# A state-space layer on VectorE: the next group's product with B placed in front of the last scan

## The chip, the cores and the metric

The kernel runs on one core of one Trainium2 chip. The metric is the device time of one execution in microseconds (us). Before the change it is 19662.92 us, the median of three runs (19660.62 to 19663.58).

## The reference, cut to what matters

The network has four layers, each added to its input after a group norm. The change touches only layer 1, which runs two mamba blocks one after the other over 65536 positions (256 x 256), for two images with 64 channels each, 128 inner channels and 16 states:

```python
dA = jnp.exp(jnp.einsum('bld,dn->bldn', delta, A))
dBu = jnp.einsum('bld,bln,bld->bldn', delta, Bm, u)

def step(h, xs):
    dA_t, dBu_t, C_t = xs
    h = dA_t * h + dBu_t
    return (h, jnp.einsum('bdn,bn->bd', h, C_t))
...
y = jnp.moveaxis(ys, 0, 1) + u * D
y = y * _silu(res)
return y @ out_w.T
```

`delta` is a softplus and `u` a Silu of a short convolution. A layer norm follows each block.

## The kernel before, in words

**Steps and groups.** The positions are cut into 128 chunks of 512. A step is one chunk of one mamba block: the list `tasks` alternates the two blocks, the second one three chunks behind the first, and has 256 steps. Within a step there are eight groups (b, j), for the two images b and four state indices j. A group holds four tiles `h[:, k]` of 128 x 512: channels and states are laid out so that one j covers all 128 channels with four of the 16 states. The text calls the groups of a step g0 to g7: g0 to g3 are b=0 with j=0 to 3, g4 to g7 are b=1.

**What a group does.**
- The product with B, delta times u times B, fills `h`. For j = 0, 1 and 3 VectorE makes it (L773) from `dv` (delta times u, fetched from DRAM) and `pb`, a PSUM bank in which TensorE has spread the row of B over the partitions. For j = 2 GpSimd makes it (L755, function `product`) from `cb`, a copy of the B and C rows in SBUF; this is issued at the end of the group three earlier, at j = 3.
- For k = 0 to 3 ScalarE computes `da = exp(delta * A)` into PSUM (L789), and VectorE scans `h[:, k]` in place with it (L792). `da` has three buffers.
- GpSimd keeps the last column as the next state (L795) and multiplies `h` by C (L796).
- TensorE sums over the states into the bank `py` (the matmuls `py<-h`); the function `before` issues these in the fourth scan's place (k = 3) of the following group. `py` has one bank and starts for each half with `u * D`.
- `gate` (L654, VectorE) multiplies `py` of a finished half with `silu(res)`. It is issued in the groups with j = 1, that is in g1 for the second half of the step before and in g5 for the first half of this one.

**What stands around it.** The engines' order is written out by hand (a manual schedule)[...]. At k = 3 of each group, ahead of the fourth `da`, the generator `steps` issues one part of the work for other steps: the front end of the step two ahead (`front`: affine in g0, convolution matmuls in g1 and g2, Silu activations in g3, the matmuls for delta and B, C in g4, softplus, the copy of B and C, GpSimd's `du` (L622) and the spill to DRAM in g5), the fetches of the next step (L641, L645, in g1 and g5), and the layer norm of the step before (`layer_norm`: out projection, square and mean in g6, logarithm and exponential in g7; its VectorE product L673 comes in the next g0, batch statistics of the second block in g1). Exponential, Silu, softplus and logarithm need different activation tables, so ScalarE reloads tables in g3, g5 and g7.

**The bank pb.** `spread` issues the TensorE matmul that fills `pb` for the next direct group, right behind the product that used it:

```python
def spread():
    n, b, j = next(rows, (None, None, None))
    if n is None:
        return None
    pb = p_b.tile([P, T], F32, name="pb")
    mm(pb, sel[:, b, j], ts[n]["bc"])
    return pb
```

`pb` has one bank, `h` five buffers, `dl`, `dv` and `cb` three each. In the profile all these matmuls stand under the helper's line, L561, and are told apart by their tiles.

## Time and profile before

| | |
|---|---|
| median of three runs | 19662.92 us |
| the profiled execution, its own time | 19667.66 us |
| its span | 19665.9 us |
| first to last L773 (layer 1) | 1533.4 to 15696.1 us |
| scans L792 | 8192, 1263 ns each |
| VectorE products L773 | 1536, 2261 ns each |
| gates L654 | 512, 684 ns each |
| exponentials L789 | 8192, 688 ns each |
| GpSimd products L796 / L755 | 2048, 4518 ns / 512, 4529 ns |

The page lists each engine's busy time as a share of the span. In rows of waits the engine and line that waited come first, then what it waited for, the total in us, the number of times and the longest. In the timeline each row has its start, its length, the engine, line and operation with its tiles, how many instructions it joins, and in brackets the idle time before it and what ended it. Start-to-start times are a little shorter than lengths where instructions of one engine overlap.

### The profile page before, as it was taken

The numbers are of one execution on the slowest core, as the hardware profiler recorded it, in microseconds if no ns is written. First come the engines' busy times: TensorE is split into PE (matmuls) and PEld (weight loads), VectorE is DVE, ScalarE is ACT, GpSimd is POOL, SyncE is SP. The second block draws the span as 40 slices with busy tenths as digits, with TensorE's granted clock in tenths as the row PEclk, the third lists the DMA queues.
The fourth block names the chain that finished last, engine by engine and source line by source line (L and its number), as shares of the span: only waits on it lengthen the run. The fifth ranks groups of instructions, "written<-read, shape, count | busy, mean of one in ns | idle before, by whom it ended". The sixth has DMA issues, their size and how long they took to land. (4 is left out here: it accounts for less than half of the span.)

```text
span 19665.9 us, 162715 instructions
## 1 busy us (share of the span) xinstructions
PE 14640.5 (74%) x48720; PEld 4861.7 (25%) x48720; DVE 18472.7 (94%) x16222; ACT 11804.0 (60%) x16810; POOL 16050.1 (82%) x8070
## 2 busy tenths in 40 slices
PE   7996767776777677767777677676777688888886
PEld 3431111111111111111111111111111154444444
DVE  6888999999999999999999999999999989999997
ACT  2226666666666666666666666666666555555554
POOL 6987888888888888888888888888888855555554
PEclk9996666666666666666666666666666698989898
DMA  3116666666666666666666666666666500000004
GB/s 124 54 50 157 151 151 151 153 149 156 149 154 152 151 151 151 155 147 157 151 153 150 151 152 151 156 148 154 154 150 151 126 28 29 30 30 29 29 27 145
DMA packets 662182, 2438.84 MB, mean 124 GB/s; under 512 B 131888, under 2 KB 201264, under 8 KB 450160
## 3 DMA queue, kind: packets, MB, share of 16 engines
q1 hardware_dynamic: 661296, 2428.43, 51.4%
q8 instruction: 385, 6.31, 0.1%
q14 instruction: 501, 4.10, 0.1%
HBM read 1990.14 MB, written 437.78 MB: 123 GB/s over the span
## 5 line engine op out<-in xcount | busy, mean ns | idle before, releaser
L792 DVE TENSOR_TENSOR_SCAN h<-da,st,h 128x512 f32<-128x512 f32 x8192 | 9838.6, 1263 | 308.2 <-ACT da L789 223.3
L796 POOL TENSOR_TENSOR h<-h,cb 128x2048 f32<-128x2048 f32 x2048 | 9253.1, 4518 | 164.9 <-POOL st L795 0.4
L789 ACT ACTIVATE da<-dl,p_a 128x512 f32<-128x512 f32 x8192 | 5565.3, 688 | 3985.5 <-DVE h L792 3891.2
L561 PE MATMUL py<-h,t_c_quad 128*32 128x512 f32 x16384 | 3253.7, 817 | 1649.1 <-POOL h L796 1648.6
L561 PE MATMUL pb<-bc,t_c_sel 64*128 64x512 f32 x3072 | 2697.0, 972 | 2385.5 <-DVE h L773 2379.9
L773 DVE TENSOR_TENSOR h<-dv,pb 128x2048 f32<-128x2048 f32 x1536 | 3472.3, 2261 | 40.9 <-DMA dv<-d_dv 40.9
L1021 POOL TENSOR_TENSOR gl<-gl,prod 128x512 f32<-128x512 f32 x1544 | 1959.0, 1270 | 1498.7 <-ACT prod L1017 1423.3
L755 POOL TENSOR_TENSOR h<-dv,cb 128x2048 f32<-128x2048 f32 x512 | 2318.7, 4529 | 17.1 <-DMA dl<-d_dl 17.1
L980 DVE SCALAR_TENSOR_TENSOR acc<-z,tap_b,acc 128x1024 f32<-128x1024 f32 (+1 forms) x1560 | 1988.4, 1275 | 38.8
L561 PEld LDWEIGHTS pb<-bc,t_c_sel 64*128 64x128 f32 x3072 | 661.6, 267 | 4411.3 <-DVE h L773 4345.9
L795 POOL COPY st<-h 128x4 f32<-128x4 f32 x2048 | 384.1, 188 | 1365.1 <-DVE h L792 1352.7
L561 PEld LDWEIGHTS py<-h,t_c_quad 128*32 128x32 f32 x16384 | 424.0, 122 | 3815.3 <-POOL h L796 3217.3
L561 PE MATMUL mm<-xin,p_conv 64*128 64x512 f32 x4096 | 1322.9, 775 | 15.2 <-DMA x1t<-y 15.2
L1064 PE MATMUL pcv<-z,diag 128*128 128x512 f32 x2322 | 1174.7, 623 | 19.8 <-ACT gl L1072 16.4
L949 ACT COPY z<-pz 128x512 f32<-128x512 f32 x768 | 456.4, 598 | 1034.1 <-PE pz L941 928.7
L1017 ACT ACTIVATE prod<-z,tap_a 128x512 f32<-128x512 f32 x1544 | 1045.1, 714 | 37.0 <-POOL gl L1021 36.8
L941 PE MATMUL pz<-t_c_inv,gf 128*128 128x128 f32 (+1 forms) x8192 | 1039.4, 309 | 1.9 <-DVE gf L922 1.9
L941 PEld LDWEIGHTS pz<-t_c_inv,gf 128*128 128x128 f32 (+1 forms) x8192 | 849.4, 181 | 520.0 <-issue 311.7
L561 PE MATMUL mm<-u,p_dt 128*128 128x512 f32 x1024 | 931.2, 1064 | 0.0
L561 PE MATMUL py<-u,p_d 128*128 128x512 f32 x1024 | 820.8, 894 | 0.0
L915 PE MATMUL f<-t_w_inT,xf 64*128 64x384 f32 x2048 | 596.7, 616 | 155.9 <-DVE gf L922 154.8
L561 PEld LDWEIGHTS mm<-xin,p_conv 64*128 64x128 f32 x4096 | 460.5, 244 | 982.6 <-issue 982.5
(167 smaller groups left out, 17448.8 us busy)
## 6 DMA issues: line engine op xcount, KB each, us to landing
cb<-d_bc SPq DMA_DIRECT2D x2048, 320.0 KB
dl<-d_dl SPq DMA_DIRECT2D x2048, 256.0 KB
dv<-d_dv SPq DMA_DIRECT2D x2048, 256.0 KB
d_dl<-delta SPq DMA_DIRECT2D x256, 512.0 KB
d_dv<-du SPq DMA_DIRECT2D x256, 512.0 KB
xin<-in_x SPq DMA_DIRECT2D x16, 2048.0 KB
xt<-in_x SPq DMA_DIRECT2D x32, 1024.0 KB
y<-yt SPq DMA_DIRECT2D x128, 256.0 KB
```

Of the source, the lines that this page charges most:

```text
L561: nc.tensor.matmul(out, lhsT, rhs, start=start, stop=stop)
L755: nc.gpsimd.tensor_tensor(h, t["dv", b], t["cb", b][:, 0].unsqueeze(1).to_broadcast([P, 4, T]), ALU.mult,)
L773: nc.vector.tensor_tensor(h, t["dv", b], pb.unsqueeze(1).to_broadcast([P, 4, T]), ALU.mult)
L789: nc.scalar.activation(da, t["dl", b][:, k], AF.Exp, scale=ws[m]["a"][:, k, j : j + 1])
L792: nc.vector.tensor_tensor_scan(h[:, k], da, h[:, k], state[m, b][:, j, k : k + 1], ALU.mult, ALU.add)
L796: nc.gpsimd.tensor_tensor(h, h, t["cb", b][:, 1 + j].unsqueeze(1).to_broadcast([P, 4, T]), ALU.mult)
L915: nc.tensor.matmul(p, x_f[t][half, g], w_in[half], start=True, stop=True)
L941: nc.tensor.matmul(pz[i * n : (i + 1) * n, k, :, 16 * g : 16 * g + 16], gf[t, 2 * e + g, b][:, c0 : c0 + n], inv, start=True, stop=True,)
L980: eng.scalar_tensor_tensor(out, near(s, name, m0, r, k), w, box["t"], ALU.mult, ALU.add)
L1017: nc.scalar.activation(prod, near(s, name, 4 * h + m, n, k), AF.Copy, scale=w)
L1021: nc.gpsimd.tensor_add(acc, acc, prod)
L1064: nc.tensor.matmul(box["t"], diag[:, k], near(s, f"a{i}", 4 * h + m, n, k), start=k == 0, stop=k == 8,)
```

## The change

The direct product of a group moves from the head of its own group to the group before it, between the fourth `da` and the fourth scan. It becomes a function, `direct_product`, that also issues the next `spread`; its tile is handed on in the dictionary `ahead`, which the products of j = 2 use already. Groups with j = 1 are followed by j = 2, so nothing is moved into them. The gate moves from the head of the groups with j = 1 to the place in front of their third exponential and scan. On TensorE, the matmuls for `pb` so come behind the `py` matmuls that `before` issues at k = 3. What is computed stays the same.

```diff
--- before.py
+++ after.py
@@ -760,27 +760,29 @@
                     )
                     return h

-                ahead = {2: product(*groups[2])}
+                def direct_product(n, b, j):
+                    nonlocal pb
+                    h = pool.tile([P, 4, T], F32, name="h", bufs=5)
+                    nc.vector.tensor_tensor(
+                        h, ts[n]["dv", b], pb.unsqueeze(1).to_broadcast([P, 4, T]), ALU.mult
+                    )
+                    pb = spread()
+                    return h
+
                 pb, before = spread(), None
+                ahead = {2: product(*groups[2]), 0: direct_product(*groups[0])}
                 for g, (n, b, j) in enumerate(groups):
                     if b == j == 0:
                         steps = aside(n)
                     if j == 0:
                         st = states.tile([P, 4, 4], F32, name=f"st{tasks[n][0]}{b}")
                     t, m = ts[n], tasks[n][0]
-                    if j != 2:
-                        h = pool.tile([P, 4, T], F32, name="h", bufs=5)
-                        nc.vector.tensor_tensor(
-                            h, t["dv", b], pb.unsqueeze(1).to_broadcast([P, 4, T]), ALU.mult
-                        )
-                        pb = spread()
-                    else:
-                        h = ahead.pop(g)
+                    h = ahead.pop(g)
                     if b == j == 0:
                         next(norm, None)
-                    if j == 1 and g > 1:
-                        gate(ts[n - 1 + b], 1 - b)
                     for k in range(4):
+                        if j == 1 and k == 2 and g > 1:
+                            gate(ts[n - 1 + b], 1 - b)
                         if k == 3:
                             next(steps)
                             if before:
@@ -789,6 +791,8 @@
                         nc.scalar.activation(
                             da, t["dl", b][:, k], AF.Exp, scale=ws[m]["a"][:, k, j : j + 1]
                         )
+                        if k == 3 and g + 1 < len(groups) and j != 1:
+                            ahead[g + 1] = direct_product(*groups[g + 1])
                         nc.vector.tensor_tensor_scan(
                             h[:, k], da, h[:, k], state[m, b][:, j, k : k + 1], ALU.mult, ALU.add
                         )
```

## The prediction

> **What bounds the kernel now.** I read the page's busy times first, then the waits inside layer 1 (1533 to 15715 us), then the timeline engine by engine. The page:

> ```profile
> PE 14640.5 (74%) x48720; PEld 4861.7 (25%) x48720; DVE 18472.7 (94%) x16222; ACT 11804.0 (60%) x16810; POOL 16050.1 (82%) x8070
> ```

> VectorE (DVE) is the bound; GpSimd (POOL) is near it. What VectorE waits for in layer 1:

> ```profile
> DVE h L792 <- ACT da L789: 223.3, 357, 1.1
> DVE res L654 <- PE py L561: 202.8, 237, 7.0
> ```

> So about 430 us is all that better order inside VectorE could win. [...] Between the first and last of 254 steps VectorE took (15648.56 - 1642.17) / 253 = 55.36 us a step. One step on VectorE, then ScalarE (ACT), POOL and PE:

> ```profile
> 8015.11 2.26 DVE L773 TENSOR_TENSOR h<-dv,pb 128x2048 f32<-128x2048 f32 x1
> 8017.29 0.68 DVE L654 TENSOR_TENSOR res<-res,py 128x512 f32<-128x512 f32 x1
> 8017.89 9.50 DVE L792 TENSOR_TENSOR_SCAN h<-da,st,h 128x512 f32<-128x512 f32 x8
> 8033.96 1.28 DVE L792 TENSOR_TENSOR_SCAN h<-da,st,h 128x512 f32<-128x512 f32 x1 [0.66 <-ACT da L789]
> 8035.16 2.26 DVE L773 TENSOR_TENSOR h<-dv,pb 128x2048 f32<-128x2048 f32 x1
> 8037.53 4.81 DVE L792 TENSOR_TENSOR_SCAN h<-da,st,h 128x512 f32<-128x512 f32 x4
> 8042.25 2.26 DVE L773 TENSOR_TENSOR h<-dv,pb 128x2048 f32<-128x2048 f32 x1
> 8045.51 0.69 DVE L654 TENSOR_TENSOR res<-res,py 128x512 f32<-128x512 f32 x1 [1.00 <-PE py L561]
> 8046.12 9.50 DVE L792 TENSOR_TENSOR_SCAN h<-da,st,h 128x512 f32<-128x512 f32 x8
> ```

> ```profile
> 8042.37 0.69 ACT L789 ACTIVATE da<-dl,p_a 128x512 f32<-128x512 f32 x1 [0.48 <-DVE h L792]
> 8043.08 1.28 ACT L525 ACT_TABLE_LOAD   x1
> 8046.12 1.28 ACT L789 ACT_TABLE_LOAD   x1
> 8047.43 0.69 ACT L789 ACTIVATE da<-dl,p_a 128x512 f32<-128x512 f32 x1
> ```

> ```profile
> 8035.58 4.52 POOL L796 TENSOR_TENSOR h<-h,cb 128x2048 f32<-128x2048 f32 x1
> 8040.05 4.53 POOL L755 TENSOR_TENSOR h<-dv,cb 128x2048 f32<-128x2048 f32 x1
> 8044.79 4.51 POOL L796 TENSOR_TENSOR h<-h,cb 128x2048 f32<-128x2048 f32 x1
> 8049.26 2.36 POOL L622 TENSOR_TENSOR du<-delta,u 128x1024 f32<-128x1024 f32 x1
> 8051.83 4.50 POOL L796 TENSOR_TENSOR h<-h,cb 128x2048 f32<-128x2048 f32 x1
> ```

> ```profile
> 8056.39 1.94 PE L561 MATMUL py<-h,t_c_quad 128*32 128x512 f32 x8 [1.56 <-POOL h L796]
> 8058.25 2.07 PE L561 MATMUL pb<-bc,t_c_sel 64*128 64x512 f32 x2
> ```

> The waits stand at fixed places. The scan's wait is in the last scan of g3 (165 us of it over the 254 steps), behind ScalarE's Silu work; the rest (56 us) lies in g6. The gate's (194 us) is in g5. The step's other gate, in g1, waits once.

> [...] a direct product D (L773) is followed by its own scan 2.37 us after its start (8035.16, 8037.53), but by the gate, which doesn't read it, after 2.18. [...] in the trace da always waits behind the side work. [...] the pb pair shows both, 2.07 and 1.12 us. [...]

> **The change, part by part.** Nothing is added or removed: a step keeps 32 scans, six D, two gates. Start-to-start on VectorE: scan 1.18 ((9.50 - 1.26) / 7), D 2.18 or 2.37, gate 0.60 (8017.29 to 8017.89), layer-norm product 0.60 likewise, batch statistics 0.60 in every second step (0.30 on average).

> *D in front of the last scan.* Its own scan no longer follows, so each costs 2.18. Before, three of six paid 2.37 (those of g3, g4, g7; others had a gate or L673 behind). Worth 0.57 us a step if nothing waits.

> *Which group has the D as cover.* Between the last scan of a group (s3) and the next s3 stood that group's own D; now it is the next group's. So g2 and g6 gain a D of cover, g1 and g5 lose theirs. ScalarE's da is a ring of three, so its third da waits for the previous s3, and the side work and fourth da come after it. In g5 the side work is the softplus with two table loads. Counted from s3 of g4 (8042.25 - 1.18 = 8041.07), da for the last scan is ready at 8048.15, that is 7.08 later. New VectorE work in that stretch: four scans and the gate, 4.72 + 0.60 = 5.32. New wait 1.76 us. In g3 the Silu side work needs 7.83 (s3 of g2 at 8027.31 - 1.18 = 8026.13, last scan 8033.96) against 6.90: wait 0.93, which eats the 0.19 there. g6 and g7 have 6.90 and need less: ScalarE's side work of g7, from the load of L670 at 8056.37 to the end of L671's activation at 8060.29, makes it about 2.0 + 3.9 + 0.7 = 6.6.

> *The gate two scans down.* py waits for POOL and PE. From s3 of g3 the gate now comes at 6.90 + 3.54 = 10.44 us; POOL's product ends at 6.14 and PE then needs 2 to 4 us at most. The wait goes: 0.76 a step, and 0.08 of overlap that a wait costs.

> *pb and PE's order.* The bank pb is single, and PE loads the next pb behind the D. That matmul was issued at the group's start, ahead of the py matmuls of the group before; now it is issued at the fourth scan, right behind them, and those wait for POOL. The place where it bites is D for the next g0, now in g7: its pb stands behind py of g5. POOL's queue from s3 of g3 is back to back (product, L755, product, du, product: rows above) and ends at 8056.33, 22.37 us after that s3; over 252 steps it lies between 22.35 and 22.39. VectorE can't change it, since POOL starts on s3 of g3 and the inputs come in time. Then py 1.94 and pb 2.07, at the slow clock, which pb had there in all 252: ready at 26.36, D at 26.44 with the 0.08 that the gate showed behind its matmul. Queued behind D: s3 of g7, and behind that POOL. Buffers h (five) are no limit: each D reuses one whose group ended at least two groups before. DMA issues aren't moved; dv is fetched most of a step ahead.

> Walk, t=0 at s3 of g3: D in g4 at 4.72, s3 of g4 6.90; s3 of g5 13.98 (7.08, ScalarE); s3 of g6 20.88; D in g7 would go at 25.60 and goes at 26.44; s3 of g7 28.62; g0 +0.60 +6.90 = 36.12; g1 +5.32 +0.30 = 41.74; g2 +6.90 = 48.64; g3 +7.83 = 56.47. Against 55.36 this is +1.11 us, times 256 = +284 us. Check of the same sums on before: 32 x 1.18 + 3 x 2.37 + 3 x 2.18 + 1.2 + 0.6 + 0.3 = 53.5, waits with overlap 0.74 + 0.84 + 0.25: 55.3.

> The profiled execution, 19667.7 with a span of 19665.9, would be 19952; it lies 4.7 us above the median, 19662.9, which gives **19947**.

> **Rivals.**
> 1. *PE fast at pb.* With pb at 1.12 and py at 1.07 it is ready at 24.6, no wait at D: step 25.60 + 30.03 = 55.63, +0.27, **19732**. For: PE reached the fast clock at py of g4 in many steps. Against: pb at this place never did.
> 2. *Own scan after D isn't what costs 2.37.* Then the three D in front of s3 of g7, g0 and g2 take 0.19 more each, +0.57: **20093**. Against: gate and L673 both start 2.18 after D.
> 3. *Run-ahead hides it (not slower).* ScalarE is idle 40% and PE 26%; if they run far enough ahead at g5 and at D of g7, my two waits (1.76 + 0.84 = 2.60) vanish: 52.94 + 0.93 = 53.87, -1.49 a step, **19282**. It decides where the two sum to less than 1.34 us (faster) or 1.64 (no change). Against: the ring of three da and the single pb allow no more.

> **How the numbers follow.** Forecast as walked 0.67 (19905 to 20020[...]); rival 1 0.14; rival 2 0.08; rival 3 0.08, 0.05 of it faster and 0.03 no change; a larger loss, say a D late elsewhere, 0.03. The range 19720 to 20100 takes in the forecast and rivals 1 and 2. Rival 1, at +0.36%, can touch no change: 0.02 moved there. Faster 0.05, same 0.05, slower 0.90; 0.2% is about what a measurement of this kernel can tell from none.

> **What would show it.** L654 waits for PE near zero; L792 waits for da about (0.85 + 1.68) x 256 = 650 us, in g3 and g5; L773, which has one wait now (a DMA at the start), waits for PE's pb about 0.76 x 256 = 195 us, all in g7; POOL idle grows. Wrong if D never waits for pb (rival 1), if the scan after D keeps 2.37 (rival 2), or if da waits stay at 223 us (rival 3).

## The result, and the profile after

The changed kernel takes 19809.58 us (median, 19805.36 to 19813.92), the kernel before 19663.25 us: a ratio of 1.0075, with a 95% interval of 1.006 to 1.009. It is slower by 146 us, 0.57 us for each of the 256 steps. The forecast had the sign, and was 137 us too high; the time lies inside the stated range.

The engines' busy times on the page of the changed kernel:

```profile
PE 14857.8 (75%) x48720; PEld 4840.9 (24%) x48720; DVE 18401.4 (93%) x16222; ACT 11710.9 (59%) x16810; POOL 16045.6 (81%) x8070
```

VectorE has the same number of instructions and about the same work, spread over a longer span. Its waits in layer 1 (columns: total us, times, longest):

```profile
DVE h L796 <- ACT da L791: 652.1, 511, 1.8
DVE h L766 <- PE pb L561: 64.6, 105, 0.7
...
DVE res L654 <- PE py L561: 7.0, 1, 7.0
```

The scan is now L796, the exponential L791, the direct product D L766. The gate's wait went from 202.8 to 7.0 us. The scan's wait for `da` went from 223.3 to 652.1, and D waits for `pb`, which it never did before. One step on VectorE, from D in g4 on:

```profile
8105.21 2.26 DVE L766 TENSOR_TENSOR h<-dv,pb 128x2048 f32<-128x2048 f32 x1
8107.39 3.63 DVE L796 TENSOR_TENSOR_SCAN h<-da,st,h 128x512 f32<-128x512 f32 x3
8110.94 0.66 DVE L654 TENSOR_TENSOR res<-res,py 128x512 f32<-128x512 f32 x1
8111.52 1.27 DVE L796 TENSOR_TENSOR_SCAN h<-da,st,h 128x512 f32<-128x512 f32 x1
8114.47 4.81 DVE L796 TENSOR_TENSOR_SCAN h<-da,st,h 128x512 f32<-128x512 f32 x4 [1.68 <-ACT da L791]
8119.20 2.26 DVE L766 TENSOR_TENSOR h<-dv,pb 128x2048 f32<-128x2048 f32 x1
8121.38 4.80 DVE L796 TENSOR_TENSOR_SCAN h<-da,st,h 128x512 f32<-128x512 f32 x4
8126.56 2.29 DVE L766 TENSOR_TENSOR h<-dv,pb 128x2048 f32<-128x2048 f32 x1 [0.38 <-PE pb L561]
```

The gate (8110.94) no longer waits. The last scan of g5 (8114.47) waits 1.68 us instead. On ScalarE the same stretch shows why:

```profile
8108.70 0.69 ACT L791 ACTIVATE da<-dl,p_a 128x512 f32<-128x512 f32 x1 [2.68 <-DVE h L796]
8109.41 1.28 ACT L525 ACT_TABLE_LOAD   x1
...
8112.45 1.28 ACT L791 ACT_TABLE_LOAD   x1
8113.75 2.74 ACT L791 ACTIVATE da<-dl,p_a 128x512 f32<-128x512 f32 x4
```

The third `da` of g5 starts only once the last scan of g4 has released a buffer, after 2.68 us in which ScalarE stood still behind D. The softplus follows with two table loads of 1.28 us each, of the six that ScalarE makes in a step, and the fourth `da` starts at 8113.75. Over 253 steps the distances between the D's stand beside the walk of the prediction like this:

| from D to D | walk, us | measured mean, us |
|---|---|---|
| g0's D1 to g2's D3 | 12.52 | 12.49 |
| D3 to g3's D4 | 6.90 | 6.90 |
| D4 to g4's D5 | 7.83 | 7.85 |
| D5 to g6's D7 | 13.98 | 13.97 |
| D7 to g7's D0 | 7.74 | 7.19 |
| D0 to D1 | 7.50 | 7.51 |

(A D is named here by the group whose `h` it fills.) Five of the six terms are right to 0.03 us. The sixth holds the whole error, 0.55 us times 256 = 141 us. The matmuls for `pb` of that D were slow in the step above (2.07 us), and fast in the next (1.16):

```profile
8115.87 1.93 PE L561 MATMUL py<-h,t_c_quad 128*32 128x512 f32 x8 [3.09 <-POOL h L800]
8122.92 1.60 PE L561 MATMUL py<-h,t_c_quad 128*32 128x512 f32 x8 [1.33 <-POOL h L800]
8124.44 2.07 PE L561 MATMUL pb<-bc,t_c_sel 64*128 64x512 f32 x2
...
8172.32 1.94 PE L561 MATMUL py<-h,t_c_quad 128*32 128x512 f32 x8 [3.08 <-POOL h L800]
8179.37 1.94 PE L561 MATMUL py<-h,t_c_quad 128*32 128x512 f32 x8 [0.38 <-POOL h L800]
8181.24 1.16 PE L561 MATMUL pb<-bc,t_c_sel 64*128 64x512 f32 x2
```

In 102 of the 253 steps this pair took 1.9 us or more, and D waited in each; in 151 it was fast (1.12 to 1.20 us), and D waited in none.

### The profile page after: what moved, and what is told of

It is laid out like the page before. It is cut to its first block, busy times and chain, and to the rows that moved or that the text cites. A ratio compares the mean times of both kernels' runs of the same rounds, so it can differ in the third digit from the quotient of the medians.

```text
span 19806.7 us, 161182 instructions
## 1 busy us (share of the span) xinstructions
PE 14857.8 (75%) x48720; PEld 4840.9 (24%) x48720; DVE 18401.4 (93%) x16222; ACT 11710.9 (59%) x16810; POOL 16045.6 (81%) x8070
## 5 line engine op out<-in xcount | busy, mean ns | idle before, releaser
L796 DVE TENSOR_TENSOR_SCAN h<-da,st,h 128x512 f32<-128x512 f32 x8192 | 9894.5, 1262 | 652.2 <-ACT da L791 652.1
L791 ACT ACTIVATE da<-dl,p_a 128x512 f32<-128x512 f32 x8192 | 5492.2, 686 | 4210.6 <-DVE h L796 4132.0
L561 PE MATMUL py<-h,t_c_quad 128*32 128x512 f32 x16384 | 3166.3, 843 | 2781.4 <-POOL h L800 2779.7
L766 DVE TENSOR_TENSOR h<-dv,pb 128x2048 f32<-128x2048 f32 x1536 | 3472.4, 2261 | 104.6 <-PE pb L561 64.6
L561 PE MATMUL pb<-bc,t_c_sel 64*128 64x512 f32 x3072 | 2553.2, 923 | 19.3 <-DVE h L766 19.3
L755 POOL TENSOR_TENSOR h<-dv,cb 128x2048 f32<-128x2048 f32 x512 | 2315.1, 4522 | 16.1 <-DMA cb<-d_bc 16.1
L561 PE MATMUL py<-u,p_d 128*128 128x512 f32 x1024 | 915.4, 991 | 973.0 <-DVE res L654 973.0
L561 PEld LDWEIGHTS py<-h,t_c_quad 128*32 128x32 f32 x16384 | 389.7, 124 | 4980.6 <-POOL h L800 4656.1
L561 PE MATMUL mm<-xin,p_conv 64*128 64x512 f32 x4096 | 1362.4, 796 | 15.4 <-DMA x1t<-y 15.4
L561 PEld LDWEIGHTS pb<-bc,t_c_sel 64*128 64x128 f32 x3072 | 630.5, 255 | 1972.2 <-DVE h L766 1100.0
L561 PE MATMUL mm<-u,p_dt 128*128 128x512 f32 x1024 | 787.5, 913 | 0.0
L561 PEld LDWEIGHTS mm<-xin,p_conv 64*128 64x128 f32 x4096 | 470.6, 249 | 990.1 <-issue 989.9
```

The lines of the kernel that those rows point to most:

```text
L561: nc.tensor.matmul(out, lhsT, rhs, start=start, stop=stop)
L755: nc.gpsimd.tensor_tensor(h, t["dv", b], t["cb", b][:, 0].unsqueeze(1).to_broadcast([P, 4, T]), ALU.mult,)
L766: nc.vector.tensor_tensor(h, ts[n]["dv", b], pb.unsqueeze(1).to_broadcast([P, 4, T]), ALU.mult)
L791: nc.scalar.activation(da, t["dl", b][:, k], AF.Exp, scale=ws[m]["a"][:, k, j : j + 1])
L796: nc.vector.tensor_tensor_scan(h[:, k], da, h[:, k], state[m, b][:, j, k : k + 1], ALU.mult, ALU.add)
```

## The experiments

### One part alone

The D moved, the gate left at the head of its group:

```diff
+if j == 1 and g > 1:
+    gate(ts[n - 1 + b], 1 - b)
 for k in range(4):
-    if j == 1 and k == 2 and g > 1:
-        gate(ts[n - 1 + b], 1 - b)
```

> The changed kernel with the gate back at the head of the j=1 groups. Theory (the last scan of g5 waits for ScalarE's softplus work whatever stands before it): py is ready about 7.5 us after s3 of g3 and the gate would come at 8.1, so it waits little, and what it would wait comes out of the 1.68 us wait for da behind it: 19,790 to 19,830, as the changed kernel. Rival (the gate's place itself is worth the 0.8 us a step that it waited before): 19,980 or more.

Measured 19845.77 us (ratio to before 1.0093, 1.0078 to 1.0108): 16 us above the range of the theory, and far below the rival, which falls. The gate waits 19.2 us in all, so the move of D alone takes nearly all of its wait away. In g5 the gate's place costs nothing: from the last scan of g4 to that of g5 it is 7.08 us in this run and in the changed kernel. The 36 us between the two lie elsewhere: the last scan of g3 waits 16 us more, and D's wait for `pb` rose from 64.6 to 85.4 us. What makes these two grow is not shown, and the two intervals of the ratio overlap.

The gate moved, the D left at the head of its own group:

```diff
-if j == 1 and g > 1:
-    gate(ts[n - 1 + b], 1 - b)
 for k in range(4):
+    if j == 1 and k == 2 and g > 1:
+        gate(ts[n - 1 + b], 1 - b)
```

> The kernel before with only the gate moved two scans down. Theory: the gate's wait for py, 0.84 us a step, goes, but the D of g1 and g5 is then followed by its own scan (2 x 0.19 more), and the last scan of g6 comes earlier while ScalarE's square still waits for PE's out projection, about 0.3 more: 19,590 to 19,640. Rival (the whole gate wait is won): about 19,450.

Measured 19474.15 us (0.9905, 0.9888 to 0.9921): 188 us faster than before, 116 us below my range and near the rival's number, though not for the rival's reason. The waits of VectorE show what I had missed; this is the whole wait for `da`, and it lies in g3:

```profile
DVE h L792 <- ACT da L789: 170.4, 258, 0.8
```

I had expected the wait in g6 to grow, and it went. The PE rows of g5 and g6 say why:

```profile
8070.70 1.13 PE L561 MATMUL py<-u,p_d 128*128 128x512 f32 x2 [0.94 <-DVE res L654]
8072.35 1.07 PE L561 MATMUL py<-h,t_c_quad 128*32 128x512 f32 x8 [0.52 <-POOL h L796]
8073.35 1.08 PE L561 MATMUL mm<-res,p_out 128*64 128x512 f32 x4
```

The later gate starts the next `py` later, so PE stands still for 0.52 us ahead of py of g4, not 1.2 to 2.6 (before) or 2.1 to 3.1 (changed). Both that py and the out projection behind it then run fast (means of 1.07 and 1.08 us over the steps between 5000 and 8000 us; 1.93 and 1.94 in the changed kernel), and ScalarE's square no longer comes late. The sum, with this: -0.84 (gate's wait) -0.25 (g6) +0.38 (two D's followed by their own scans) = -0.71 a step, -182 us.

So the two parts are worth +183 (D) and -188 us (gate), and together +146. They don't add up, since each alone takes away nearly all of the gate's wait (19.2 and 7.0 us are left) and of the 56 us that the scan waited in g6, and these can be won only once. Against that, the +0.38 a step of the gate alone doesn't arise where D is moved too.

### The wait in g5

The D of g5 back at the head of g5, all else as changed:

```diff
+if g not in ahead:
+    ahead[g] = direct_product(n, b, j)
 h = ahead.pop(g)
 ...
-if k == 3 and g + 1 < len(groups) and j != 1:
+if k == 3 and g + 1 < len(groups) and j != 1 and (b, j) != (1, 0):
```

> The changed kernel with the D of g5 back at the head of g5, so that the softplus work of g5 has its cover again. Theory with the pin: the da wait of g5 (427 us) goes, but s3 of g6 then comes early at 19.3 us after s3 of g3 and waits for ScalarE's square, which waits for PE's out projection behind py of g4 and so for GpSimd's queue (about 20.6), and D of g7 for pb as now: a gain of 0.2 to 0.4 us a step only, 19,700 to 19,770, with a new da wait of about 1.3 us in g6. Rival (the da wait of g5 alone costs the time): 1.57 us a step are won, about 19,410.

Measured 19790.91 us (1.0066, 1.005 to 1.0081), a little above the range of the first theory and far from the rival. It is above because D's wait for `pb` did not stay as it was. The largest wait of the changed kernel is gone, and 19 us are won. VectorE's waits and a step from D of g5 on:

```profile
DVE h L798 <- ACT da L793: 506.1, 505, 1.5
DVE h L766 <- PE pb L561: 145.9, 161, 2.3
```

```profile
8047.29 2.26 DVE L766 TENSOR_TENSOR h<-dv,pb 128x2048 f32<-128x2048 f32 x1
8049.65 2.46 DVE L798 TENSOR_TENSOR_SCAN h<-da,st,h 128x512 f32<-128x512 f32 x2
8052.03 0.66 DVE L654 TENSOR_TENSOR res<-res,py 128x512 f32<-128x512 f32 x1
8052.61 5.97 DVE L798 TENSOR_TENSOR_SCAN h<-da,st,h 128x512 f32<-128x512 f32 x5
8058.50 2.26 DVE L766 TENSOR_TENSOR h<-dv,pb 128x2048 f32<-128x2048 f32 x1
8061.95 1.28 DVE L798 TENSOR_TENSOR_SCAN h<-da,st,h 128x512 f32<-128x512 f32 x1 [1.19 <-ACT da L793]
```

g5 runs through without a wait, and the last scan of g6 (8061.95) waits 1.19 us for the `da` behind ScalarE's square, which stands behind PE's out projection and py of g4, and so behind GpSimd. What remains is lost in g7, at `pb`. Removing one wait let the next in the chain end last.

### The wait for pb

In g6, `pb` made ahead of the py matmuls of g5:

```diff
 if k == 3:
     next(steps)
-    if before:
+    if before and (b, j) != (1, 2):
         before()
 ...
     ahead[g + 1] = direct_product(*groups[g + 1])
+if k == 3 and (b, j) == (1, 2):
+    before()
```

> The changed kernel, in which PE in g6 makes pb for the next step's first group before the py matmuls of g5, not behind them. Theory: the waits of D for pb (64.6 us and 0.08 each) go, nothing else moves: 19,720 to 19,750. Rival (that D waits because GpSimd or the D before it is late): no change, 19,810.

Measured 19730.92 us (1.0035, 1.0021 to 1.0048), as expected: 79 us won, and of the D's wait this is left:

```profile
DVE h L766 <- PE pb L561: 0.2, 1, 0.2
```

PE's order alone made that wait: `pb` still takes 1.9 us or more in 135 of 253 steps, but is ready in time. Both edits together:

> The D of g5 at home and, in g6, pb before the py matmuls of g5. Theory: D of g7 no longer waits for pb (145.9 us in 161 times, with 0.08 each), s3 of g6 still waits for ScalarE's square at about 20.6 us: 19,610 to 19,660. Rival (without the pb wait VectorE only waits longer in g6 or g7): about 19,790.

Measured 19620.52 us (0.9978, 0.9969 to 0.9987), as expected, and the first version with the D's moved that is below the kernel before. Its D's don't wait for `pb`; the scans still wait 497.8 us for `da`.

### Why pb was often fast

Before the change, `pb` at this place was slow (2.07 us) in all of 253 steps. It followed a py of g4 that was often fast (median 1.36 us, after 1.2 to 2.6 us of pause). After it, with 2.1 to 3.1 us of pause, py of g4 is slow (1.93) in all 253, and `pb` mostly fast. To turn this round, PE's pause in g5 was filled with needless matmuls:

```diff
 d(1)
+fill = p_mm.tile([P, T], F32, name="mm")
+for _ in range(2):
+    mm(fill, ws[tasks[n][0]]["d"], t["u"][:, 1])
```

> The changed kernel with two needless products of 128x512 added on PE in g5 behind the start of py, into a bank that nobody reads, where PE stands still for about 3 us before py of g4. Theory (a pause of that length makes py of g4 and the out projection slow, and PE, busier for it, is fast again at pb): py of g4 takes 1.07 instead of 1.93, and pb of g7 is slow again in nearly all steps, so D waits for it 150 to 200 us in place of 65: 19,880 to 19,940. Rival (more work on PE only keeps it fast): pb fast in all steps, no D wait, 19,740.

Measured 19886.63 us (1.0113, 1.0098 to 1.0128), in the range of the theory: with these two products more in g5, `pb` was slow in more steps. A step on PE, and the D that waits for it:

```profile
8034.04 2.72 PE L561 MATMUL mm<-u,p_d 128*128 128x512 f32 x4
8036.69 1.07 PE L561 MATMUL py<-h,t_c_quad 128*32 128x512 f32 x8
8037.69 1.08 PE L561 MATMUL mm<-res,p_out 128*64 128x512 f32 x4
8039.52 1.13 PE L561 MATMUL mm<-lsq,mean 128*128 128x512 f32 x2 [0.76 <-ACT lsq L662]
8043.51 1.93 PE L561 MATMUL py<-h,t_c_quad 128*32 128x512 f32 x8 [2.85 <-POOL h L803]
8045.37 2.07 PE L561 MATMUL pb<-bc,t_c_sel 64*128 64x512 f32 x2
```

```profile
8047.48 2.29 DVE L769 TENSOR_TENSOR h<-dv,pb 128x2048 f32<-128x2048 f32 x1 [0.73 <-PE pb L561]
```

With the pause filled, py of g4 is fast (median 1.07), PE then stands still longer ahead of py of g5 (median 2.88 us, not 1.33), and `pb` takes 1.9 us or more in 216 of 253 steps, not in 102. D waits 128.7 us in 200 steps, not 64.6 in 105. That is below the 150 to 200 us I gave, and `pb` is slow in most steps, not in nearly all.

### A version that beats both

The runs say what to keep: two D's of cover in g3, whose Silu work is the longest (7.83 us against 7.08 in g5); one in g5, g6 and g7; none in g2 and g4; the gate where the change puts it; `pb` ahead of py in g6; and py of g4 held back until then, so that the out projection doesn't wait for GpSimd:

```diff
-pb, before = spread(), None
+pb, before = spread(), lambda: None
+held, AHEAD = [], ((0, 0), (0, 3), (1, 2), (1, 3))
 ...
+if g not in ahead:
+    ahead[g] = direct_product(n, b, j)
 h = ahead.pop(g)
 ...
-    if before:
-        before()
+    held.append(before)
+    if b == 0 or j in (0, 3):
+        while held:
+            held.pop(0)()
 ...
-if k == 3 and g + 1 < len(groups) and j != 1:
+if k == 3 and g + 1 < len(groups) and (b, j) in AHEAD:
     ahead[g + 1] = direct_product(*groups[g + 1])
+if k == 3 and (b, j) == (1, 2):
+    while held:
+        held.pop(0)()
```

> D moved in front of the last scan in g0, g3, g6 and g7 only, at the head of its own group for g3 and g5; gate two scans down; in g6 pb before py, and py of g4 held back until then, so that the out projection doesn't stand behind it. Theory: g3 has two D of cover (9.27 against 7.83), g5 one (7.69 against 7.08), g6 and g7 one each (6.90), no wait is left: 53.3 us a step, 19,120 to 19,250. Rival (GpSimd's queue, which needs about 50 us a step, still holds VectorE somewhere): 19,400 or more.

Measured 19129.56 us (0.9728, 0.9714 to 0.9743): 534 us, 2.7%, faster than before. A step takes 53.26 us against the 53.3 expected. The busy times, and VectorE's only wait of layer 1 between 1700 and 15000 us:

```profile
PE 14460.3 (76%) x48720; PEld 4837.7 (25%) x48720; DVE 18382.2 (96%) x16222; ACT 11768.3 (62%) x16810; POOL 16045.9 (84%) x8070
```

```profile
DVE h L804 <- DVE h L766: 1.8, 4, 0.5
```

The same without holding back py of g4 (in g5 it is issued at k = 3 as ever):

```diff
-    if b == 0 or j in (0, 3):
+    if (b, j) != (1, 2):
```

> The recut order without holding back py of g4: the out projection stands behind it again. Theory: s3 of g6 would come at 19.3 us and waits for ScalarE's square until 20.7 where PE is slow at py of g4: 1.0 to 1.4 us a step above the run with py held back, 250 to 360 us, nearly all as a da wait in g6. Rival (py of g4 isn't what the out projection waits for): the same time as with it held back.

Measured 19445.28 us (0.9889, 0.9874 to 0.9904), 316 us more, as expected, and nearly all of it is this wait, once a step:

```profile
DVE h L804 <- ACT da L796: 296.9, 256, 1.8
```

So in this order the place of one py in PE's queue is worth 316 us, more than twice the whole effect of the change studied.

## Why the prediction was right or wrong

The parts add up: +428.8 us for the scan's wait for `da`, +64.6 for D's wait for `pb`, -195.8 for the gate's wait, and -146 for D's that no longer stand ahead of their own scan (0.57 us in 256 steps) make +151.6, against +146 measured. The direction, the scan's wait and the gate's are as forecast; D's wait for `pb` was put at about 195 us, and the size of the whole is about half. The time lies outside the band of the forecast as walked (19905 to 20020), and inside the range only because that took in rival 1 too; a mix of the two was not worked out, so that part was luck.

- *The gate's wait goes*: right, 202.8 to 7.0 us, the rest being one wait at the layer's end.
- *g5 loses its cover, and its last scan waits 1.76 us*: right (0.08 of it is the overlap that a wait costs, since a scan takes 1.26 us and the next starts 1.18 after its start; the wait itself is 1.68). About 650 us of waits for `da` were forecast, in g3 and g5, and 652.1 came, in 511 waits. The place is confirmed by giving g5 its D back.
- *A D not followed by its own scan costs 2.18*: right, 8105.21 to 8107.39, and 2.18 in the median of the 1272 D's behind which nothing waits; the scan that follows there reads another group's `h`. A D that is followed by its own scan still costs 2.36, 8047.29 to 8049.65 in the run with D of g5 at home, as in 765 D's before the change (median 2.37). Rival 2 falls.
- *GpSimd pins py of g5 at 22.37 us*: right; in the changed kernel GpSimd's product for g5 ends 22.36 to 22.40 us after the last scan of g3 starts.
- *"Then py 1.94 and pb 2.07, at the slow clock, which pb had there in all 252"*: this is the term that was mis-sized. The wait was right: D waits for `pb` where it is slow, and putting `pb` first removes the wait. But `pb` was slow in 102 of 253 steps only, so that D lost 0.29 us a step in the mean and not 0.84. I carried PE's speed in the old order over into the new one, though the change moves the D and the gate, and so the start of PE's work, just ahead of that stretch. Rival 1, at 0.14, was true for 151 of 253 steps; the measured time lies between it and the forecast.
- *Rival 3, run-ahead hides it*: falls. The sum of the two waits had to be below 1.34 us to win; the one in g5 alone was larger.

## What to carry to other kernels

A long instruction on the bounding engine, as here D with its 2.26 us, is also cover for what other engines do meanwhile: before moving it, list for each stretch between two synchronising points how much side work hides there, and count that stretch again without it. When one wait is removed, ask which chain ends next, since the next one can stand just behind: here, with VectorE busy 93% of the span and GpSimd 81%, 425 us of waits in g5 were taken away, and 19 us were won. And where one engine makes both, move what the bounding engine needs ahead of what waits for a slow engine: PE made `pb` behind py in all 253 steps of the changed kernel, and issuing it ahead of py won 79 us.

## What the runs showed of the hardware that was not expected

- PE's speed at one place changed with what it had done shortly before, and not as one would guess. After a pause of 2.1 to 3.1 us py of g4 took 1.93 us, and 8.0 to 8.9 us after its start `pb` was fast (1.12 instead of 2.07) in 151 of 253 steps. With the pause filled, py took 1.07 in the median, and `pb` was slow in 216 steps. In which steps it was slow went also with the place on the grid of 3.41 us on which the granted clock changes: in the changed kernel 1 of 104 steps in one part of the interval, and all 72 in another. How much load goes with which clock is not shown.
- A VectorE product followed by a scan that reads it costs 0.19 us more than one followed by another instruction (medians of 2.37 and 2.18 us from start to start, over 765 products before the change and 1272 after), also where that other instruction is a scan as well. Over three products in each of 256 steps that is 146 us, as much as the change itself.
